# Two graph layers in one kernel: the second layer's weights, the sums of product 2 and the transpositions and projections of x in other places

## The chip, the cores and the metric

The kernel runs on one core of a Trainium2 chip. The metric is the time of one execution on the device in microseconds (us); several executions are taken and their median is given. A core has five engines that run their own instruction streams and wait for one another through semaphores: TensorE (PE; its weight loads are listed apart, as PEld), VectorE (DVE), ScalarE (ACT), GpSimd (POOL) and SyncE (SP), which here only issues DMA. SBUF is the memory on the core, PSUM the small one that PE writes its products to.

## What is computed

x has 16 batches of 1024 nodes and 64 channels, adj is 1024 x 1024; all is 32-bit floating point. Cut to what matters, the reference is:

```python
# layer 0
Q = einsum('bnc,oc->bno', x, Wq) + bq
K = einsum('bnc,oc->bno', x, Wk) + bk
V = einsum('bnc,oc->bno', x, Wv)
score = softmax(einsum('bnc,bmc->bnm', Q, K), axis=1)
score = einsum('bnm,mc->bnc', score, adj)
x = layernorm(x + einsum('bnm,bmc->bnc', score, V))
# layer 1, with support = adj twice
x1 = einsum('ij,bjk->bik', adj, x)
x2 = 2.0 * einsum('ij,bjk->bik', adj, x1) - x
out = concatenate([x, x1, x2, x1, x2], -1) @ weight + bias
x = layernorm(x + out)
```

The kernel multiplies adj with x first (the score matrix is then applied to that product), so there are three large products with adj: one ahead of the attention and two in layer 1. Since layer 1 uses the same support twice, its weights can be added up in front: that is `layer_weights`.

## The kernel before

**Products with adj.** Each large product is a Strassen product: seven products of half the size, numbered 1 to 7, with sums of blocks formed on DVE. Products 2, 3 and 4 are themselves cut into seven parts (`PARTS`, in the order 1, 2, 6, 5, 7, 3, 4). Sums that are needed later stand in a list, `line`; `fill(n)` emits the next n of them, `need(name)` all up to the last with that name. The order in which instructions are emitted is the order in which each engine runs its own. `step` is one half of a product of half the size, `part` one of the seven parts; both emit PE's matmuls, then some sums, then the reading of the PSUM tile.

```python
line = []

def later(name, pieces):
    line.extend((name, piece) for piece in pieces)

def fill(n):
    for _ in range(min(n, len(line))):
        line.pop(0)[1]()

def need(*names):
    while any(name in names for name, _ in line):
        fill(1)
# ... cut ...
    def read(self, name, g, rows=(0, 1)):
        pt = self.tiles[g if name in (1, 6, 7, 4) else 2 + g]
        for i, c in self.targets(name):
            self.take(
                pt[:, rows[0] * H : (rows[-1] + 1) * H],
                i * HB + 2 * g + rows[0], len(rows), c * NP // 2, NP // 2,
            )

    def step(self, name, g, fills=0, rows=(0, 1)):
        self.matmuls(name, g, rows)
        fill(fills)
        self.read(name, g, rows)
# ... cut ...
    def part(self, name, q, two_tiles, fills=1):

        a, b = self.sub[q]
        tile_, bank = {1: (0, 0), 6: (0, 0), 7: (0, 0), 4: (0, 0), 2: (1, 0)}.get(q, (1, 1))
        pt = two_tiles[tile_][:, ts(bank, H)]
        start = q in (1, 2, 5)
        W = H // 2
        for i in range(2):
            for k in range(2):
                nc.tensor.matmul(
                    pt[:, ts(i, W)], a[:, k, ts(i, P)], b[:, :, k],
                    start=(start and i == k == 0), stop=(k == 1), skip_group_check=True,
                )
        fill(fills)
        (i, c), = self.targets(name)
        di, dc = {1: (0, 0), 2: (0, 0), 6: (0, 1), 3: (0, 1), 7: (1, 1), 5: (1, 1), 4: (1, 0)}[q]
        self.take(pt, i * HB + 2 * di, 2, c * NP // 2 + 2 * dc, 2)
```

A reading adds to the result on DVE if the result's block has been written before, and copies on ACT if not. Products 5 and 7 have two targets each, so both engines read the tile.

```python
    def take(self, pt, block, n, pair, m):

        got = pt.rearrange("p (i q f) -> p q i f", i=n, q=m)
        cells = {(block + i, pair + q) for i in range(n) for q in range(m)}

        def at(t):
            return t[:, pair : pair + m, block : block + n]

        assert cells <= self.seen or not cells & self.seen
        if cells <= self.seen:
            nc.vector.tensor_add(at(self.res), got, at(self.res))
        elif self.plus is None:
            nc.scalar.activation(at(self.res), got, AF.Copy)
        else:
            nc.vector.tensor_add(at(self.res), got, at(self.plus))
        self.seen |= cells
```

**Transpositions, projections and weights.** The scores of layer 0 need x transposed (xT) and a projection of it (GY), for each of eight pairs of batches. Both go through a PSUM tile that ACT evicts.

```python
def transposed(p, pt=None):

    pt = ps_tile("pt") if pt is None else pt
    for k in range(K8):
        nc.tensor.transpose(pt[:, ts(k, P)], xs[:, p, k, :], ident)
    nc.scalar.activation(xT[:, p], pt, AF.Copy)

def score_weight(pw):
    nc.tensor.transpose(pw[:, 0:P], wq, ident)
    nc.tensor.transpose(pw[:, P : 2 * P], wk, ident)
    nc.vector.tensor_copy(wn, pw[:, 0 : 2 * P].rearrange("p (a o) -> p a o", a=2))

def score_weight_2(pm):
    nc.tensor.matmul(pm[:, 0:P], wn[:, 1], wn[:, 0], start=True, stop=True)
    nc.tensor.matmul(pm[:, H : H + 1], wn[:, 0], bkp, start=True, stop=True)
    nc.vector.tensor_copy(m_w, pm[:, 0:P])
    nc.vector.tensor_copy(gb, pm[:, H : H + 1])

def rows_of(p):
    return xs[:, p].rearrange("p k (b c) -> p (k b) c", b=2)

def project(p, pg=None):
    pg = ps_tile("pg") if pg is None else pg
    for h in range(2):
        nc.tensor.matmul(pg[:, ts(h, H)], m_w, xT[:, p, ts(h, H)], start=True, stop=True)
    nc.scalar.activation(GY[:, p], pg, AF.Identity, bias=gb, scale=1.0)
# ... cut ...
def layer_weights():
    w24 = const.tile([P, C], FP, tag="w24", name="w24")
    nc.vector.tensor_add(w24, w1s[:, 2], w1s[:, 4])
    nc.vector.tensor_sub(raw[:, 0], w1s[:, 0], w24)
    nc.vector.tensor_add(raw[:, 0], raw[:, 0], ident[:, 0:C])
    nc.vector.tensor_add(raw[:, 0], raw[:, 0], ident[:, C:P])
    nc.vector.tensor_add(raw[:, 1], w1s[:, 1], w1s[:, 3])
    nc.vector.tensor_scalar(raw[:, 2], w24, 2.0, None, op0=ALU.mult)
    rsum = const.tile([P, 5], FP, tag="rsum", name="rsum")
    nc.vector.tensor_reduce(rsum, raw, AX.X, ALU.add)
    nc.vector.scalar_tensor_tensor(
        raw, rsum[:, :, None].to_broadcast([P, 5, C]), -1.0 / C, raw, op0=ALU.mult, op1=ALU.add
    )
    wv = pair_weight("wv")
    for j in range(2):
        s = slice(j * C, (j + 1) * C)
        nc.vector.tensor_copy(wv[s, s], raw[s, 3])
    return wv
```

**The attention.** It takes 64 steps, eight for each of eight pairs of batches. `scores(n)` fills two PSUM tiles and DVE evicts them with their row maxima; ACT takes the exponentials; `scaled` divides the rows of the product of adj by the sums; `weighted` multiplies on PE. PSUM tiles of the pool `ps` come from three buffers in turn.

```python
const = ctx.enter_context(tc.tile_pool(name="const", bufs=1))
big = ctx.enter_context(tc.tile_pool(name="big", bufs=1))
small = ctx.enter_context(tc.tile_pool(name="small", bufs=4))
ps = ctx.enter_context(tc.tile_pool(name="ps", bufs=3, space=bass.MemoryType.PSUM))
pacc = ctx.enter_context(tc.tile_pool(name="pacc", bufs=1, space=bass.MemoryType.PSUM))
# ... cut ...
def scores(n):

    p, m = steps[n]
    sc = [ps_tile(f"sc{j}") for j in range(2)]
    for h in range(2):
        for j in range(2):
            s = slice(j * C, (j + 1) * C)
            nc.tensor.matmul(
                sc[j][:, ts(h, H)], GY[s, p, ts(m, P)], xT[s, p, ts(h, H)],
                start=True, stop=True,
            )
    NM[n] = small.tile([P, 2], FP, tag="nm", name="nm")
    E[n] = att.tile([P, 2, N], FP, tag="e", name="e", bufs=3)
    for j in range(2):
        nc.vector.tensor_scalar(
            E[n][:, j], sc[j], -1.0, None, op0=ALU.mult, op1=ALU.min,
            accum_out=NM[n][:, j : j + 1],
        )
    SM[n] = small.tile([P, 2], FP, tag="es", name="es")

def exponentials(n, j):
    nc.scalar.activation(
        E[n][:, j], E[n][:, j], AF.Exp, bias=NM[n][:, j : j + 1], scale=-1.0,
        accum_out=SM[n][:, j : j + 1],
    )

def scaled(n):

    p, m = steps[n]
    ri = small.tile([P, 2], FP, tag="ri", name="ri")
    nc.vector.reciprocal(ri, SM.pop(n))
    US[n] = small.tile([P, 2, C], FP, tag="us", name="us")
    nc.vector.tensor_tensor(
        US[n], U[:, m, ts(p, P)].rearrange("p (b c) -> p b c", b=2),
        ri[:, :, None].to_broadcast([P, 2, C]), ALU.mult,
    )

def weighted(n):
    p, m = steps[n]
    if m == 0:
        ACC[p] = pacc.tile([P, N], FP, tag="acc", name="acc")
    es, us = E.pop(n), US.pop(n)
    for h in range(2):
        for j in range(2):
            nc.tensor.matmul(
                ACC[p][j * C : (j + 1) * C, ts(h, H)], us[:, j], es[:, j, ts(h, H)],
                start=(m == 0), stop=(m == K8 - 1),
            )
```

```python
def centre(p):
    nc.gpsimd.tensor_tensor(
        rows_of(p), rows_of(p), mu[:, p, :, None].to_broadcast([P, G, C]), ALU.subtract
    )
```

**The main sequence**, as far as the change touches it. Of PSUM there are four tiles of two banks, h0 to h3 (`h`); `two` is h2 and h3.

```python
for n in (1, 2, 4):
    later(f"S{n}", left_sum(S, n))
for q in PARTS:
    first.part(2, q, two, {1: 0, 3: 2, 4: 2}.get(q, 1))
need("T1", "S1")
first.step(5, 0, 8)
need("S4")
later("half", both(*first.halves(3, room[0])))
first.step(5, 1, 8)
need("half")
later("T2", first.right_sum(2))
later("T3", first.right_sum(3))
later("S3", left_sum(S, 3))
for q in PARTS:
    first.part(3, q, two)
score_weight(h[3])
transposed(0, h[2])
need("T2")
lefts, rights = first.halves(4, room[1])
later("half", lefts)
later("mu", [
    lambda p=p: nc.vector.tensor_reduce(mu[:, p], rows_of(p), AX.X, ALU.add)
    for p in range(NP)
])
first.step(6, 0, 5)
score_weight_2(h[3])
transposed(1, h[2])
first.step(6, 1, 6)
project(0, h[3])
transposed(2, h[2])
need("S3", "T3")
line[:0] = [("T4", f) for f in first.right_sum(4)]
first.step(7, 0, 6)
project(1, h[3])
transposed(3, h[2])
line[:0] = [("half", f) for f in rights]
first.step(7, 1, 6)
project(2, h[2])
project(3, h[3])
need("T4", "half")
for q in PARTS:
    first.part(4, q, two)
    if q == 6:
        scores(0)
        for j in range(2):
            exponentials(0, j)
need("mu")
nc.vector.tensor_scalar(mu, mu, 1.0 / C, None, op0=ALU.mult)
nc.sync.dma_start(aT[:, low, right], a_in[:, low, right])
scores(1)
for j in range(2):
    exponentials(1, j)
transposed(4)
scaled(0)
wv = layer_weights()
for p in range(5):
    centre(p)
# ... cut ...
last = len(steps) - 1
for n, (p, m) in enumerate(steps):
    if (p, m) == (NP - 2, 2):
        later("half", both(*hop_1.halves(2, room[0])))
    if n + 2 <= last:
        scores(n + 2)
        exponentials(n + 2, 0)
    if p and m > 4:
        weigh(p - 1, m - 5)
    elif p > 1 and m == 0:
        weigh(p - 2, 3)
    elif p == 0 and m:
        if m % 2:
            project(m // 2 + 4)
        else:
            transposed(m // 2 + 4)
            centre(m // 2 + 4)
    if n + 1 <= last:
        scaled(n + 1)
    if m <= 4:
        fill(1)
    weighted(n)
    if m == K8 - 1:
        take(p)
    if n + 2 <= last:
        exponentials(n + 2, 1)
```

Of the kernel before, what the change touches and what calls it, by code (L numbers as in the profile page):

```python
# [18 lines left out]
def gnn_kernel(  # L19
# [31 lines left out]
    def ps_tile(name):  # L51
        return ps.tile([P, 2 * H], FP, tag="ps", name=name)
# [7 lines left out]
    def pair_weight(name):  # L60
        w = const.tile([P, P], FP, tag=name, name=name)
        nc.vector.memset(w, 0.0)
        return w
# [44 lines left out]
# [26 lines that stand above are left out]
# [14 lines left out]
# [18 lines that stand above are left out]
# [52 lines left out]
    def by_pair(t):  # L218

        return t.rearrange("p k (q f) -> p q k f", f=P)  # L220
# [4 lines left out]
# [10 lines that stand above are left out]
# [159 lines left out]
# [36 lines that stand above are left out]
# [19 lines left out]
# [4 lines that stand above are left out]
# [20 lines left out]
    def weigh(p, c, pw=None):  # L473

        pw = (ps_tile("pw") if pw is None else pw).rearrange("p (b f) -> p b f", b=2)
# [4 lines that stand above are left out]
                    pw[:, j, ts(k, 3 * C)], xT[s, p, ts(2 * c + k, P)],  # L480
                    raw[s, 0:3].rearrange("p w c -> p (w c)"), start=True, stop=True,
                )
        to = pw[:, :, 0 : 6 * C].rearrange("p b (k w c) -> p w k b c", k=2, w=3)
        blocks = slice(2 * c, 2 * c + 2)

        def at(t):
            return t[:, p].rearrange("p (k b c) -> p k b c", k=K8, b=2)[:, blocks]

        nc.scalar.activation(at(GY), to[:, 2], AF.Copy)  # L489
        nc.vector.tensor_tensor(  # L490
            at(xT), to[:, 0], raw[:, 4:5, None].to_broadcast([P, 2, 2, C]), ALU.add
        )
        nc.scalar.activation(
            U[:, blocks, ts(p, P)].rearrange("p k (b c) -> p k b c", b=2), to[:, 1], AF.Copy
        )

    def both(lefts, rights):
        return [f for pieces in zip(lefts, rights) for f in pieces]

    S = left_tiles()  # L500
    h = [ps_tile("h0"), ps_tile("h1"), pacc.tile([P, N], FP, tag="acc", name="h2"), ps_tile("h3")]
    two = h[2:]
    first = Product(S, xs, by_pair(U), h, None, (2, 3, 4))
# [7 lines left out]
    for n in (1, 2, 4):  # L511
        later(f"S{n}", left_sum(S, n))
    for q in PARTS:
        first.part(2, q, two, {1: 0, 3: 2, 4: 2}.get(q, 1))
    need("T1", "S1")
    first.step(5, 0, 8)
    need("S4")
# [6 lines left out]
    for q in PARTS:  # L524
        first.part(3, q, two)
    score_weight(h[3])
    transposed(0, h[2])
    need("T2")
    lefts, rights = first.halves(4, room[1])
    later("half", lefts)  # L530
# [2 lines left out]
        for p in range(NP)  # L533
    ])
    first.step(6, 0, 5)
    score_weight_2(h[3])
    transposed(1, h[2])
    first.step(6, 1, 6)
    project(0, h[3])
    transposed(2, h[2])  # L540
    need("S3", "T3")
    line[:0] = [("T4", f) for f in first.right_sum(4)]
    first.step(7, 0, 6)
    project(1, h[3])
    transposed(3, h[2])
    line[:0] = [("half", f) for f in rights]
    first.step(7, 1, 6)
    project(2, h[2])
    project(3, h[3])
    need("T4", "half")  # L550
# [11 lines left out]
        exponentials(1, j)  # L562
    transposed(4)
    scaled(0)
    wv = layer_weights()
    for p in range(5):
        centre(p)

# [7 lines left out]
# [8 lines that stand above are left out]
        elif p > 1 and m == 0:  # L584
            weigh(p - 2, 3)
        elif p == 0 and m:
            if m % 2:
                project(m // 2 + 4)
            else:
                transposed(m // 2 + 4)  # L590
                centre(m // 2 + 4)
        if n + 1 <= last:
            scaled(n + 1)
        if m <= 4:
# [6 lines that stand above are left out]
        if p:  # L601
            if m == 0:
                norm_1(p - 1)
            elif m == 1:
                norm_2(p - 1)
            elif m == 4:
                transposed(p - 1)
# [7 lines left out]
    h = [pacc.tile([P, N], FP, tag="acc", name="h0")] + [ps_tile(f"h{n}") for n in (1, 2, 3)]  # L615
# [8 lines left out]
    two = (h[2], h[3])  # L624
# [18 lines left out]
    two = (h[1], h[3])  # L643
# [136 lines left out]
```

## Time and profile before

| what | before |
|---|---|
| time, median of 3 runs | 621.12 us (620.71 to 621.95) |
| span of the profiled execution | 619.2 us |
| PE busy | 599.2 us (97%) |
| PE's weight loads busy | 305.0 us (49%) |
| DVE busy | 412.8 us (67%) |
| ACT busy | 232.8 us (38%) |
| POOL busy | 85.8 us (14%) |
| mean granted clock of PE | 0.986 |
| chain that ended last | PE 86%, DVE 6%, DMA 4%, ACT 2% |

How to read it. The profile is one execution, recorded by the hardware profiler. It has the busy time of each engine; the span in 40 equal slices, with a digit for the busy tenths of each engine and the clock that PE was granted; the chain of waits, followed back from the last instruction to what released each; groups of instructions by line; what each engine waited for (engine, tile, line, who was waited for, then us in total, times, longest); and a timeline. "L150" is line 150 of the kernel, and a line can be that of a helper: L299 and L301 are the two readings in `take`, L312 the matmuls of `step`, L375 those of `part`, L112 and L113 a transposition and its eviction, L132 and L133 a projection and its eviction, L401 and L408 the scores and their eviction, L415 the exponentials, L424 and L426 `scaled`, L438 `weighted`, L450 `centre`, L532 the sums for mu, L150 to L164 `layer_weights`. Matmuls in 32-bit floats stand in the trace as two instructions each. The share of busy time is a mean over stages with different limits, so a change is judged in its own stage.

### The profile page before, as it was taken

How to read it: one execution, taken by the hardware profiler on the slowest of the kernel's cores; microseconds unless marked ns; L12 is line 12 of the kernel's file. 1: busy time of each engine (PE TensorE's matmuls, PEld its weight loads, DVE VectorE, ACT ScalarE, POOL GpSimd, SP SyncE). 2: the span in 40 equal slices, each digit the busy share in tenths (PEclk: the TensorE clock that was granted, in tenths of full speed). 3: DMA queues.
4: the chain of work that ended last, by engine and by line, in shares of the span. 5: the costliest groups of instructions: out<-in, count | busy, mean ns of one | idle time of the engine just before them, and what ended most of it. 6: DMA issues, size and time to landing. Idle time of an engine off the chain costs nothing.

```text
span 619.2 us, 6448 instructions
## 1 busy us (share of the span) xinstructions
PE 599.2 (97%) x2478; PEld 305.0 (49%) x2478; DVE 412.8 (67%) x737; ACT 232.8 (38%) x384; POOL 85.8 (14%) x45
## 2 busy tenths in 40 slices
PE   9999999889999999999999999999999999999993
PEld 5747446423334434343443434446647466746463
DVE  0876565755586766778676787855768577648484
ACT  0111032236766667666667766662100000000111
POOL 0000000602130020303002030300000000203366
PEclk9999999969999999999999999999999999999997
DMA  8800002000000000000000000000000000000012
GB/s 264 292 7 1 0 0 69 0 0 2 1 1 1 0 1 2 1 1 0 1 2 0 2 0 1 1 1 1 1 0 0 1 0 1 1 34 35 34 68 103
DMA packets 12575, 14.34 MB, mean 23 GB/s; under 512 B 2304, under 2 KB 7424, under 8 KB 12544
## 3 DMA queue, kind: packets, MB, share of 16 engines
q1 hardware_dynamic: 12544, 13.93, 6.7%
q8 instruction: 19, 0.31, 0.2%
q14 instruction: 12, 0.10, 0.1%
HBM read 9.73 MB, written 4.19 MB: 22 GB/s over the span
## 4 chain that ended last, share of the span: by engine, by line
PE 86%; DVE 6%; DMA 4%; ACT 2%; SPq 1%; issue 1%; DVEq 0%; ACTq 0%
PE h L312 24%; PE sc L401 20%; PE acc L438 19%; PE h L375 13%; DMA xs<-in_x_dram 3%; PE pw L479 3%; PE po L458 2%; PE pt L112 2%; PE pg L132 2%; PE h L132 1%; DVE U L299 1%; DMA aT<-in_adjT_dram 1%; DVE GY L299 1%; DVE e L408 1%; PE h L112 1%; PE h L479 1%
## 5 line engine op out<-in xcount | busy, mean ns | idle before, releaser
L408 DVE TENSOR_SCALAR_CACHE_REDUCE e<-sc 128x1024 f32<-128x1024 f32 x128 | 151.7, 1222 | 64.5 <-PE sc L401 64.5
L415 ACT ACTIVATE e<-e,nm 128x1024 f32<-128x1024 f32 x128 | 146.2, 1143 | 94.7 <-DVE e L408 94.5
L401 PE MATMUL sc<-xT,GY 64*128 64x512 f32 x512 | 131.6, 621 | 4.9 <-DVE e L408 4.9
L438 PE MATMUL acc<-e,us 128*64 128x512 f32 x512 | 124.1, 605 | 0.3 <-DVE us L426 0.3
L175 POOL TENSOR_TENSOR rstd<-var,expo 128x16 f32<-128x16 f32 (+1 forms) x15 | 42.1, 2807 | 381.0 <-DVE var L170 381.0
L312 PE MATMUL h<-T,S 128*128 128x512 f32 x192 | 83.6, 593 | 0.9 <-DVE U L299 0.9
L401 PEld LDWEIGHTS sc<-xT,GY 64*128 64x128 f32 x512 | 45.7, 187 | 78.2 <-issue 46.5
L299 DVE TENSOR_TENSOR U<-h,U 128x512 f32<-128x512 f32 (+1 forms) x58 | 48.2, 837 | 53.1 <-PE h L312 30.2
L438 PEld LDWEIGHTS acc<-e,us 128*64 128x64 f32 x512 | 31.1, 136 | 70.0 <-issue 58.0
L703 ACT ACTIVATE sq<-GY 128x1024 f32<-128x1024 f32 x6 | 6.3, 1057 | 147.9 <-DVE GY L299 147.9
L312 PEld LDWEIGHTS h<-T,S 128*128 128x128 f32 x192 | 36.2, 190 | 44.5 <-issue 42.8
L312 PE MATMUL h<-S,aT 128*128 128x512 f32 x96 | 41.9, 592 | 0.0
L450 POOL TENSOR_TENSOR xs<-xs,mu 128x1024 f32<-128x1024 f32 x8 | 15.1, 1906 | 145.9 <-DVE mu L558 112.7
L375 PE MATMUL h<-xs 128*128 128x256 f32 x144 | 32.6, 382 | 1.4 <-DVE GY L299 1.1
L299 DVE TENSOR_TENSOR GY<-h,GY 128x512 f32<-128x512 f32 (+1 forms) x24 | 19.1, 798 | 16.7 <-PE h L312 11.2
L375 PEld LDWEIGHTS h<-xs 128*128 128x128 f32 x144 | 27.0, 190 | 6.2 <-DVE GY L299 1.5
L312 PEld LDWEIGHTS h<-S,aT 128*128 128x128 f32 x96 | 18.1, 190 | 22.0 <-issue 22.0
L301 ACT ACTIVATE U<-h 128x1024 f32<-128x1024 f32 x8 | 8.0, 1022 | 54.2 <-PE h L312 24.5
L479 PEld LDWEIGHTS pw<-raw,xT 64*128 64x128 f32 x224 | 19.2, 187 | 15.8 <-issue 5.8
L490 DVE TENSOR_TENSOR xT<-pw,raw 128x256 f32<-128x256 f32 x28 | 11.9, 425 | 18.6 <-ACT GY L489 18.6
L415 ACT ACTIVATION_READ_ACCUMULATOR e<-e,nm 128x1 f32 x128 | 24.0, 188 | 0.0
L479 PE MATMUL pw<-raw,xT 64*128 64x192 f32 x224 | 24.0, 332 | 0.0
(165 smaller groups left out, 625.4 us busy)
## 6 DMA issues: line engine op xcount, KB each, us to landing
xs<-in_x_dram SPq DMA_DIRECT2D x16, 256.0 KB, 5.8
aT<-in_adjT_dram SPq DMA_DIRECT2D x16, 256.0 KB, 5.5
out_dram<-GY SPq DMA_DIRECT2D x12, 256.0 KB, 2.2
aT<-in_adjT_dram SPq DMA_DIRECT2D x1, 1024.0 KB, 5.1
out_dram<-GY SPq DMA_DIRECT2D x8, 128.0 KB, 2.0
w1s<-in_w_dram SPq DMA_DIRECT2D x2, 80.0 KB, 2.7
wq<-in_wqT_dram SPq DMA_DIRECT2D x2, 16.0 KB, 4.7
wk<-in_wkT_dram SPq DMA_DIRECT2D x2, 16.0 KB, 3.8
```

Of the source, the lines that this page charges most:

```text
L112: nc.tensor.transpose(pt[:, ts(k, P)], xs[:, p, k, :], ident)
L132: nc.tensor.matmul(pg[:, ts(h, H)], m_w, xT[:, p, ts(h, H)], start=True, stop=True)
L175: nc.gpsimd.tensor_tensor(rstd, var, expo[:, 0:g], ALU.pow)
L299: nc.vector.tensor_add(at(self.res), got, at(self.res))
L312: nc.tensor.matmul(pt[:, ts(i, H)], a[:, k, ts(2 * g + i, P)], b[:, :, k], start=(start and k == 0), stop=(k == HB - 1), skip_group_check= ...
L375: nc.tensor.matmul(pt[:, ts(i, W)], a[:, k, ts(i, P)], b[:, :, k], start=(start and i == k == 0), stop=(k == 1), skip_group_check=True,)
L401: nc.tensor.matmul(sc[j][:, ts(h, H)], GY[s, p, ts(m, P)], xT[s, p, ts(h, H)], start=True, stop=True,)
L408: nc.vector.tensor_scalar(E[n][:, j], sc[j], -1.0, None, op0=ALU.mult, op1=ALU.min, accum_out=NM[n][:, j : j + 1],)
L415: nc.scalar.activation(E[n][:, j], E[n][:, j], AF.Exp, bias=NM[n][:, j : j + 1], scale=-1.0, accum_out=SM[n][:, j : j + 1],)
L438: nc.tensor.matmul(ACC[p][j * C : (j + 1) * C, ts(h, H)], us[:, j], es[:, j, ts(h, H)], start=(m == 0), stop=(m == K8 - 1),)
L450: nc.gpsimd.tensor_tensor(rows_of(p), rows_of(p), mu[:, p, :, None].to_broadcast([P, G, C]), ALU.subtract)
L479: nc.tensor.matmul(pw[:, j, ts(k, 3 * C)], xT[s, p, ts(2 * c + k, P)], raw[s, 0:3].rearrange("p w c -> p (w c)"), start=True, stop=True,)
```

## The change

It moves work and removes none.

- `layer_weights`, a dozen small instructions on DVE, goes from the beginning of the attention to a place behind the second step of product 7 of the first large product.
- In product 2 the sums that are emitted ahead of the readings go forward: two each ahead of the readings of parts 5 and 7 in place of parts 3 and 4. Their number is the same.
- The transpositions of pairs 0 to 3 go behind other steps of products 6 and 7; the projections of pairs 0 and 1 change place with some of them.
- In the steps of the first pair of the attention the transpositions of pairs 5, 6 and 7 go into steps 1, 3 and 5, and the projections of pairs 4 to 7 into steps 2, 4, 6 and 7. Before, the projections were in steps 1, 3, 5 and 7, the transpositions in 2, 4 and 6.

The aim is that small work of DVE stands where PE doesn't need DVE, and that PE meets fewer PSUM tiles that are still being read.

```diff
--- before.py
+++ after.py
@@ -511,7 +511,7 @@
     for n in (1, 2, 4):
         later(f"S{n}", left_sum(S, n))
     for q in PARTS:
-        first.part(2, q, two, {1: 0, 3: 2, 4: 2}.get(q, 1))
+        first.part(2, q, two, {1: 0, 5: 2, 7: 2}.get(q, 1))
     need("T1", "S1")
     first.step(5, 0, 8)
     need("S4")
@@ -524,7 +524,6 @@
     for q in PARTS:
         first.part(3, q, two)
     score_weight(h[3])
-    transposed(0, h[2])
     need("T2")
     lefts, rights = first.halves(4, room[1])
     later("half", lefts)
@@ -533,18 +532,20 @@
         for p in range(NP)
     ])
     first.step(6, 0, 5)
+    transposed(0, h[2])
     score_weight_2(h[3])
+    first.step(6, 1, 6)
     transposed(1, h[2])
-    first.step(6, 1, 6)
     project(0, h[3])
-    transposed(2, h[2])
     need("S3", "T3")
     line[:0] = [("T4", f) for f in first.right_sum(4)]
     first.step(7, 0, 6)
+    transposed(2, h[2])
     project(1, h[3])
     transposed(3, h[2])
     line[:0] = [("half", f) for f in rights]
     first.step(7, 1, 6)
+    wv = layer_weights()
     project(2, h[2])
     project(3, h[3])
     need("T4", "half")
@@ -562,7 +563,6 @@
         exponentials(1, j)
     transposed(4)
     scaled(0)
-    wv = layer_weights()
     for p in range(5):
         centre(p)
 
@@ -584,11 +584,11 @@
         elif p > 1 and m == 0:
             weigh(p - 2, 3)
         elif p == 0 and m:
-            if m % 2:
-                project(m // 2 + 4)
+            if m in (1, 3, 5):
+                transposed(m // 2 + 5)
+                centre(m // 2 + 5)
             else:
-                transposed(m // 2 + 4)
-                centre(m // 2 + 4)
+                project((m + 1) // 2 + 3)
         if n + 1 <= last:
             scaled(n + 1)
         if m <= 4:
```

## The prediction

> **What bounds the kernel now.** I read four views in this order: the page's 40 slices, the chain of waits, the timeline around the place that they point to, and the timeline of products 6 and 7. The slices say whether one engine is the bound and whether it keeps its clock; in the second row the clock that TensorE (PE) was granted stands in tenths.
>
> ```profile
> PE   9999999889999999999999999999999999999993
> PEclk9999999969999999999999999999999999999997
> ```
>
> PE is busy everywhere (97% of the span), so only three things can move the time: work of PE, gaps of PE, and its clock. One slice in the body of the kernel, the ninth (124 to 139 us), has a granted clock of about 0.6. The chain of work that ended last (start, length, what) passes there:
>
> ```profile
> 114.94 2.36 DVE e L408 x4
> ...
> 117.81 1.93 DVE w L150
> ...
> 119.77 1.83 DVE raw L151
> ...
> 121.69 1.76 DVE raw L152
> ...
> 125.60 1.25 DVE e L408 x2
> 126.84 0.04 issue
> 126.89 3.78 PE sc L401 x6
> 130.66 3.71 PE pg L132 x4
> 134.37 1.94 PE acc L438 x8
> 136.32 1.92 PE sc L401 x8
> 138.23 1.02 PE pt L112 x8
> 139.26 1.87 PE acc L438 x8
> 141.12 1.92 PE sc L401 x8
> 143.04 1.91 PE pg L132 x4
> ```
>
> Two things are to be seen. From 117.81 to 125.60 the chain runs through VectorE (DVE): these are the small instructions of `layer_weights`. Their place in DVE's order is ahead of the evictions of the third step's scores (e, L408). Those evictions free the PSUM buffers of the next scores, so PE stands still. Then, from 126.89, the same two PE groups that later take 1.92 and 1.91 us take 3.78 and 3.71. In stretches of the trace (length, busy time of PE, PEld, DVE, ACT, POOL, then the granted clock) this is:
>
> ```profile
> 121.60:126.90 5.30, 0.67 (x4) 0.02 (x2) 5.02 (x12) 0.03 (x1) 1.76 (x1) 0.75 0.00 0
> 126.90:134.50 7.60, 7.60 (x12) 2.52 (x14) 4.37 (x10) 3.68 (x7) 0.00 (x0) 0.50 0.00 0
> 136.25:141.05 4.80, 4.80 (x26) 2.02 (x24) 2.75 (x6) 1.86 (x5) 1.71 (x1) 1.00 0.00 0
> 141.05:146.75 5.70, 5.70 (x22) 1.85 (x20) 3.08 (x7) 4.17 (x7) 0.19 (x1) 1.00 0.01 3
> ```
>
> PE is nearly idle for 5.3 us and then works 7.6 us at half clock. The last two rows give the undisturbed beat of the first pair: 4.80 us for a step with a transposition, 5.70 for one with a projection, PE full in both. The list of what PE waited for in the whole run has only a few further entries of size; two of them are at places that the change touches:
>
> ```profile
> PE sc L401 <- DVE e L408: 4.9, 2, 4.6
> ...
> PE h L312 <- DVE U L299: 0.9, 1, 0.9
> ...
> PE h L112 <- DVE U L299: 0.6, 1, 0.6
> ```
>
> **What the Trainium skill says.** "TensorE: Matmul & The Clock Gate", Part 1 (The HAM clock gate): PE's clock falls to one half after an idle window of about 3.4 us and comes back after about as long a busy one. The trace agrees in kind: the idle stretch of some 5 us is followed by 0.50; but the half clock lasts to 134.5, that is 7.6 us of full work, longer than the page's figure. "SBUF — State Buffer", SBUF: two separate sides: a DVE instruction with two inputs in SBUF and a GpSimd (POOL) instruction reading SBUF share a port as an exclusive lock. The trace agrees: POOL runs its five `centre` instructions from 113.98 to 123.36, and L150, L151 and L152 (128x64) take 1.92, 1.82 and 1.75 us in that stretch, while L153 and L154, the same form right after it, take 0.23 and 0.22. "PSUM — Partial Sum Buffer", PSUM bank collisions: engines are to be kept from reading one bank at once, ScalarE (ACT) and DVE included. The trace agrees: in product 7 ACT's copy of a tile starts at 86.97, at the end of DVE's read of it (85.71 plus 1.23).
>
> **The change part by part.** It removes and adds no instruction; it reorders.
>
> **(a) `layer_weights` goes behind product 7's second step.** Gain: in the kernel before, the step from the scores at 121.14 to the next at 136.25 took 15.11 us and held scores, a projection and the weighted sum, 5.70 in the undisturbed beat. The loss is 15.11 - 5.70 = 9.4 us; of it 7.6/2 = 3.8 are the half clock, the rest the idle time. With the small instructions gone, DVE goes from the scaling (117.4 to 117.9) straight to the third step's scores, which PE has ready about 0.1 us after 119.27 (as the eviction at 138.26 follows PE's next start at 138.16). Two evictions of 1.15 us start to start and 1.22 long: the second buffer is free at 119.37 + 1.15 + 1.22 = 121.74, plus 0.06 to PE. PE wants it at 121.13. So a wait of about 0.65 stays, since the step before has neither transposition nor projection to fill it. Net gain 9.4 - 0.65 = 8.75. No half clock follows, as no long gap is left.
> Cost in the new place: from L153 to the end of the part the instructions took 125.60 - 123.48 = 2.1 us without POOL, and L150 to L152 add about 0.2 each, together 2.7 us in place of 7.8. After DVE's read in product 7 (95.17, next start 96.31) DVE does one sum for mu (1.21) and is then idle 3.09 until 100.61. 2.7 fits into 3.09. PE there works on projections and the last sub-product. Cost 0.
>
> **(b) Transposition 0 goes behind product 6's first step.** It stood right behind the last part of product 3, whose PSUM tile h2 it overwrites, and PE waited 0.56 for DVE's read. In the new place the read is long done, and product 6's step, which goes to h0, can start. Gain 0.56.
>
> **(c) Transposition 2 goes between product 7's first step and projection 1; transposition 3 follows and wants the same tile h2.** This makes a wait. With the old times: product 7's step ends near 85.5; DVE reads it until 86.94; ACT copies the other target from 86.97, its next instruction can start at 87.89, and that is now the eviction of transposition 2, 1.02 long, so h2 is free at 88.91. PE does transposition 2 (0.87) and projection 1 (1.72) from 85.51, so wants h2 at 88.10. Cost 0.85. ACT's copy is ahead in ACT's order, which is why the eviction can't go first. Transposition 1 and projection 0 behind product 6's second step find their buffers free.
>
> **(d) One more sum each ahead of the reads of parts 5 and 7 of product 2, one less ahead of 3 and 4.** Before the last read (part 4) two sums ran from 30.73 to 32.02, and the read began at 31.93; PE's part 4 began at 29.85 and a part takes 1.72, so the read could have begun 0.2 after 31.57, at 31.77. With one sum ahead of it DVE is waiting by then. The adjacency blocks that the earlier sums need had landed by 25.3. Gain 0.16, from the 0.94 that PE waits there; the rest of it is the end of part 4 and the read itself.
>
> **(e) Transpositions and projections of pairs 4 to 7 change places in the first pair's steps.** PE has 3 x 1.02 and 4 x 1.91 us in these seven steps in both orders; PE is the bound in them (DVE 2.75 to 3.08 us busy of 4.80 to 5.70). Worth about 0: the short transposition only meets the first step's wait earlier.
>
> Sum: 8.75 + 0.56 + 0.16 - 0.85 = 8.6 us. 621.1 - 8.6 = 612.5.
>
> **Rivals.** First, **the port lock takes the place of the wait**: `us` of the second step reads two SBUF inputs and, now earlier, falls into POOL's stretch up to 123.36, a delay of up to 1.5 us. For it: L426 took 0.47 and 0.63 beside POOL, against 0.29. Against it: PE needs `us` only after scores and a transposition, at about 124.7. If I am wrong there, another 1 us is lost: 613.5. Second, **the weights burden product 4**: if the 1.8 us of L150 to L152 were theirs and not the lock's, the part would take 7.8 us in a hole of 3.1, and the first read of product 4 would be some 4.7 late, of which PE has about 0.8 in hand; 616 or a little more, and a gap long enough to endanger the clock. The 0.23 of L153 speaks against it. Third, **the clock**: if the remaining short waits (0.3 and about 1 in the scores before, 0.65 after) together still brought the half clock, 3.8 of the gain would go, 616. PE's 0.94 wait in product 5 brought none. Fourth, **the wait of (c) doesn't come**, because ACT's order lets the eviction through earlier: 611.6.
>
> **Range and chances.** The gain of (a) is read from the trace and hardly less than 7.5; the small terms can be off by half a microsecond each, and the three runs before spread over 1.2 us. I take 611.0 to 614.5. Faster by over 2% would need 608.7, more than the whole loss that I find: 0.03. Slower by over 2% would need a new fault of 20 us: 0.01. Same: 0.96.
>
> **What would show it.** (a) The granted clock is 1.00 through the whole first pair; `layer_weights` lies near 96 to 99 us and takes about 2.7; L150 to L152 take about 0.2 each; PE's wait for e L408 falls from 4.9 to about 1. (b) No wait of L112 for U L299. (c) A new wait of PE's L112 for ACT, xT L113, of about 0.85 near 88 us. (d) PE's L312 waits for U L299 0.8 in place of 0.9. It would be wrong if the slow clock came again, or if PE waited in product 4 for DVE.

## The result, and the profile after

| | before | after |
|---|---|---|
| time, median of 4 runs | 620.99 us (620.71 to 621.95) | 612.07 us (611.82 to 612.36) |
| ratio | | 0.9854, 95% interval 0.9837 to 0.9871 |
| span of the profiled execution | 619.2 us | 610.0 us |
| PE busy | 599.2 us | 594.5 us |
| DVE busy | 412.8 us | 408.3 us |
| mean granted clock of PE | 0.986 | 0.994 |

The change made the kernel 8.9 us faster, 1.5%. In the slices of the page the ninth no longer has a lower clock; only the slow stretch at the very end is left:

```profile
PE   9999999999999999999999999999999999999993
PEclk9999999999999999999999999999999999999997
```

The chain of waits (start, length, what) at the beginning of the attention now consists of PE, but for one wait for DVE's eviction of the second scores:

```profile
115.22 1.23 DVE e L408 x2
...
116.49 1.12 PE sc L401 x2
...
117.63 1.98 PE sc L401 x6
119.61 1.87 PE acc L438 x8
121.48 1.92 PE sc L401 x8
123.40 1.02 PE pt L112 x8
```

The fourth scores begin at 121.48 and take 1.92 us in one piece, followed at once by the transposition. In the timeline of the kernel before they had begun at 121.14 and stopped after two of their eight instructions. The steps 1 and 2 together hold the same work in both kernels. The timelines give 121.14 to 141.05 before, 19.91 us, and 121.41 to 131.92 after, 10.51: 9.4 us less.

The weights stand in the timeline of DVE behind product 7's reading (start, length, line, operation):

```profile
96.59 0.22 DVE L150 TENSOR_TENSOR w<-w1s 128x64 f32<-128x64 f32 x1
...
97.17 0.23 DVE L152 TENSOR_TENSOR raw<-raw,ident 128x64 f32<-128x64 f32 x1
...
99.52 1.22 DVE L531 TENSOR_REDUCE mu<-xs 128x16 f32<-128x1024 f32 x1
100.89 0.69 DVE L299 TENSOR_TENSOR U<-h,U 128x512 f32<-128x512 f32 x1
```

L150 to L152 (L151 is left out here) take 0.22 or 0.23 us each where they took 1.75 to 1.92. The whole part takes 2.9 us (96.59 to 99.52), and the sum for mu ends at 100.74, 0.15 us ahead of the first reading of product 4. What PE waited for (us in total, times, longest):

```profile
PE h L312 <- DVE U L299: 0.8, 1, 0.8
PE h L112 <- ACT xT L113: 0.7, 1, 0.7
...
PE sc L401 <- DVE e L408: 0.3, 1, 0.3
```

The wait for e L408 fell from 4.9 to 0.3, the one of L112 for U L299 is gone, and one of L112 for ACT's eviction is new.

### The profile page after: what moved, and what is told of

Same layout as the page of the kernel before. It is cut to its first block, busy times and chain, and to the rows that moved or that the text cites. A ratio compares the mean times of both kernels' runs of the same rounds, so it can differ in the third digit from the quotient of the medians.

```text
span 610.0 us, 6448 instructions
## 1 busy us (share of the span) xinstructions
PE 594.5 (97%) x2478; PEld 303.7 (50%) x2478; DVE 408.3 (67%) x737; ACT 232.8 (38%) x384; POOL 85.8 (14%) x45
## 4 chain that ended last, share of the span: by engine, by line
PE 89%; DVE 5%; ACT 2%; DMA 2%; SPq 1%; issue 1%; DVEq 0%; ACTq 0%
PE h L312 24%; PE sc L401 20%; PE acc L438 19%; PE h L375 15%; PE pw L479 3%; PE po L458 2%; DMA xs<-in_x_dram 2%; PE pt L112 2%; PE pg L132 1%; DVE U L299 1%; PE h L132 1%; DVE GY L299 1%; SPq L77 1%; PE h L479 1%; ACT U L301 0%
## 5 line engine op out<-in xcount | busy, mean ns | idle before, releaser
L408 DVE TENSOR_SCALAR_CACHE_REDUCE e<-sc 128x1024 f32<-128x1024 f32 x128 | 151.6, 1222 | 62.7 <-PE sc L401 62.7
L401 PE MATMUL sc<-xT,GY 64*128 64x512 f32 x512 | 128.7, 615 | 0.3 <-DVE e L408 0.3
L299 DVE TENSOR_TENSOR U<-h,U 128x512 f32<-128x512 f32 (+1 forms) x58 | 48.2, 837 | 50.1 <-PE h L312 30.3
L299 DVE TENSOR_TENSOR GY<-h,GY 128x512 f32<-128x512 f32 (+1 forms) x24 | 19.1, 797 | 16.7 <-PE h L312 11.2
```

What stands on the lines that cost most here:

```text
L401: nc.tensor.matmul(sc[j][:, ts(h, H)], GY[s, p, ts(m, P)], xT[s, p, ts(h, H)], start=True, stop=True,)
L408: nc.vector.tensor_scalar(E[n][:, j], sc[j], -1.0, None, op0=ALU.mult, op1=ALU.min, accum_out=NM[n][:, j : j + 1],)
```

## The experiments

All times are medians; "before" is the kernel before in the same comparison.

| run | time | before | ratio (95%) |
|---|---|---|---|
| weights alone in the new place | 612.14 | 621.15 | 0.9847 (0.983 to 0.9864) |
| all but the weights | 621.23 | 621.15 | 1.0001 (0.9993 to 1.0009) |
| transposition 2 early | 611.36 | 621.15 | 0.9837 (0.9823 to 0.9851) |
| PE kept busy in the gap | 619.25 | 621.15 | 0.9964 (0.995 to 0.9978) |
| centring later | 612.48 | 621.23 | 0.9861 (0.9847 to 0.9874) |
| first pair in the old order | 612.00 | 621.23 | 0.9852 (0.9839 to 0.9866) |
| weights twice | 613.93 | 621.23 | 0.9886 (0.9872 to 0.9899) |
| transposition 5 in the wait | 609.83 | 621.23 | 0.9819 (0.9805 to 0.9832) |

**1. The weights alone.** The kernel before, with part (a) of the change only:

```diff
     first.step(7, 1, 6)
+    wv = layer_weights()
     project(2, h[2])
...
     scaled(0)
-    wv = layer_weights()
```

> The kernel before with one part of the change alone: the second layer's weights prepared behind product 7's second step. Theory: this part carries the whole gain, 5.3 us of standing still and 3.8 us of half clock, in all 9.4; so about 611.6 us, granted clock 1.00 in the first pair, and the small instructions of the weights at about 0.22 us each near 97 us. Rival (the parts need one another: without the transposition in step 1 and the earlier sums, a new wait for the scores' eviction takes its place): 613 to 616.

Measured: 612.14 us, 9.0 less than before. PE's waits in the first pair are down to 0.3 us and the half clock there is gone. In the chain of waits the fourth scores, which begin at 121.56, take 1.92 us again and the projection follows at once:

```profile
119.69 1.87 PE acc L438 x8
121.56 1.92 PE sc L401 x8
123.48 1.91 PE pg L132 x4
```

One moved line carries the gain, and it needs none of the other parts.

**2. All but the weights.** The changed kernel with the opposite edit, so the parts (b) to (e) alone.

> The changed kernel with the weights put back to the beginning of the attention; all else as changed. Theory: the other parts together are worth -0.56 (transposition 0) -0.15 (sums of product 2) +0.70 (wait ahead of transposition 3), about 0.0; so 621.0 us, with the half clock back for about 10 us. Rival (the short transposition in step 1 in place of a projection shortens the slow stretch): about 620, since 1.9 - 1.0 us less work falls into the half clock.

Measured: 621.23 us, with a ratio of 1.0001. The other parts cancel out, to within about half a microsecond. The stretches of this run (length, busy time of PE, PEld, DVE, ACT, POOL, then the granted clock) add something that was not expected:

```profile
121.40:126.80 5.40, 1.12 (x4) 0.29 (x2) 5.12 (x11) 0.00 (x0) 2.23 (x2) 1.00 0.00 0
126.80:133.60 6.80, 6.45 (x16) 3.03 (x18) 4.73 (x12) 4.36 (x7) 0.69 (x1) 0.50 0.00 0
```

PE stands still just as in the kernel before, but the clock falls only at 126.79, 0.4 us before PE goes on at 127.15. The clock records of the trace have it at half for 6.83 us, against 10.24 in the kernel before, whose first 2.6 us lay in the gap, where PE had no work that could become slower. So the length of the slow stretch in the record is not its cost; only the part with work in it counts, 7.6 us before and 6.5 here.

**3. Transposition 2 early.** The changed kernel, with its new wait taken away:

```diff
     project(0, h[3])
+    transposed(2, h[2])
     need("S3", "T3")
     line[:0] = [("T4", f) for f in first.right_sum(4)]
     first.step(7, 0, 6)
-    transposed(2, h[2])
     project(1, h[3])
     transposed(3, h[2])
```

> The changed kernel with transposition 2 put back ahead of product 7's first step, so that transposition 3 no longer overwrites a tile whose eviction waits behind ACT's copy. Theory: PE's wait of 0.70 us of the changed kernel goes and nothing takes its place: 611.4 us, 0.6 to 0.7 less than the changed kernel. Rival (PE then waits at the same place for product 7's reading or for projection 1's tile): 612.1, the same.

Measured: 611.36 us, and PE's wait for xT L113 is not in the list any more. Beside the changed kernel on one chip (experiment 9) the difference is 0.82 us. How the wait arose is seen in the timeline of the changed kernel:

```profile
85.45 1.02 ACT L301 ACTIVATE U<-h 128x1024 f32<-128x1024 f32 x1 [7.01 <-DVE U L299]
...
86.38 1.02 ACT L113 ACTIVATE xT<-h 128x1024 f32<-128x1024 f32 x1
...
87.45 1.09 PE L112 MATMUL h<-ident,xs 128*128 128x128 f32 x8 [0.70 <-ACT xT L113]
```

The eviction of transposition 2 stands behind ACT's copy of product 7, and that copy behind DVE's reading of the same tile. Transposition 3 can start only at 87.45, 0.05 after the eviction's end. Of the parts (b) to (e), (c) was the one that cost time.

**4. PE kept busy in the gap.** The kernel before; PE gets work without use while DVE prepares the weights:

```diff
+        if n == 0:
+            pg4 = ps_tile("pg")
+            for _ in range(20):
+                nc.tensor.matmul(pg4[:, 0:P], still, still, start=True, stop=True)
```

(The tile is then handed to projection 4, which overwrites it.)

> The kernel before, with 20 matmuls of zeros (128x128, into the tile that projection 4 overwrites later) put between the first weighted sums and the fourth scores, where PE stands still for DVE. The weights stay in their old place, so the wait stays; only PE is not idle in it. Theory: the clock fell because PE stood still; now it stays at 1.00, and the 3.8 us of half clock are saved: about 617.2 us. Rival (the half clock has another cause than this gap): 621.0, with half clock at the same place.

Measured: 619.25 us, so 1.9 less than before, half of what was expected. The clock did stay at 1.00, so the theory of its fall holds; the size came out otherwise. The chain of waits of this run shows why:

```profile
127.33 1.12 PE sc L401 x2
...
128.47 1.98 PE sc L401 x6
130.45 1.91 PE pg L132 x4
```

The scores stop a second time after two of their eight instructions, until the second eviction is over (it begins at 127.19 and takes 1.22). That is a fault of the edit. `ps` has three buffers in turn, and the tile taken early for the idle work is the third. It pushes the fourth scores on to the two buffers of the third scores, and they wait for both evictions, where those of the kernel before wait for the first only. The second stop put off the rest from 127.33 to 128.47, 1.14 us. The timeline has the step at 12.58 us (121.58 to 134.16) against 15.11 before; 15.11 - 12.58 + 1.14 = 3.7, near the 3.8 worked out for the half clock. This correction is worked out from the trace, not run.

**5. Centring later.** The kernel before, with the weights in their old place; only POOL's work is moved out of their way:

```diff
-    for p in range(5):
-        centre(p)
...
         weighted(n)
+        if n == 2:
+            for q in range(5):
+                centre(q)
```

> The kernel before, with the weights in their old place; only GpSimd's first five centring instructions are emitted two steps later, so that they no longer run beside the weights. Theory: L150 to L152 are slow because GpSimd holds the port; without it the weights take 2.7 us in place of 7.8, the scores' evictions begin near 120.5, PE waits for the second of them until about 122.9 in place of standing still to 126.9, and no half clock comes: 621.1 - 9.4 + 1.8, about 613.5 us. Rival (the small instructions are slow by themselves, or the wait is long enough for the half clock anyway): 617 to 621.

Measured: 612.48 us, 8.75 less than before, without touching the weights. The timeline of DVE, and the weight load with which PE goes on in the fourth scores:

```profile
117.70 0.22 DVE L150 TENSOR_TENSOR w<-w1s 128x64 f32<-128x64 f32 x1
...
118.29 0.23 DVE L152 TENSOR_TENSOR raw<-raw,ident 128x64 f32<-128x64 f32 x1
...
120.66 1.23 DVE L408 TENSOR_SCALAR_CACHE_REDUCE e<-sc 128x1024 f32<-128x1024 f32 x1
...
121.81 1.22 DVE L408 TENSOR_SCALAR_CACHE_REDUCE e<-sc 128x1024 f32<-128x1024 f32 x1
...
121.95 0.72 PEld L401 LDWEIGHTS sc<-xT,GY 64*128 64x128 f32 x5 [0.43 <-DVE e L408]
```

The same instructions in the same place take 0.22 and 0.23 us when POOL is not at work. (Why POOL's work makes them slow, by a shared port or otherwise, the run doesn't show.) So the root of the loss was less the place of the weights than their running beside POOL's `centre`. The fourth scores take 2.64 us in the chain of waits of this run in place of 1.92. Thus, by the traces, the weights alone in the way of PE cost 0.7 us, and beside POOL 9.4. The medians have the two remedies closer, 9.0 us gained in experiment 1 and 8.75 here, but from one comparison to the next they scatter by half a microsecond. The 1.0 us by which the run beat its expectation has the same reason as the wait that the prediction had too much (below).

**6. The first pair in the old order.** The changed kernel with part (e) undone.

> The changed kernel with the old order of transpositions and projections in the first pair's steps; all else as changed. Theory: these steps are full of PE work in either order, so 612.1 us, the same as the changed kernel. Rival (the short transposition in step 1 matters, since it comes where the evictions are late): some 0.5 to 1 us more.

Measured: 612.00 us, the changed kernel's time. Part (e) does nothing that these runs can see.

**7. The weights twice.** The changed kernel, with the load in the new place doubled:

```diff
     first.step(7, 1, 6)
+    layer_weights()
     wv = layer_weights()
```

> The changed kernel with the weights prepared twice behind product 7, so twice the load of VectorE in the new place. Theory: once, it fits into VectorE's idle time there to within a few tenths of a microsecond; the second 2.7 us come out of the first reading of product 4, which ends near 103.9 in place of 101.6, while PE wants its tile at 102.3: about 1.6 us more, 613.7 us. Rival (there is more room than that, PE is not touched): 612.1.

Measured: 613.93 us, 1.9 more than the changed kernel. PE's longest wait for a reading of DVE in the parts of products rose from 0.7 to 1.8:

```profile
PE h L375 <- DVE U L299: 3.0, 4, 1.8
```

The hole behind product 7 is deep enough for one preparation and little more. Of the 2.9 us that the second one takes, PE felt 1.9; the rest went into the 0.15 us that DVE and about 0.7 us that PE had in hand there (in the changed kernel the first reading of product 4 ends at 101.58, and PE takes the tile at 102.34).

**8. A version faster than both.** On top of experiment 3, the transposition of pair 5 goes into the wait that is left ahead of the third scores:

```diff
     scores(1)
+    transposed(4)
+    transposed(5, pacc.tile([P, N], FP, tag="acc", name="pt5"))
     for j in range(2):
         exponentials(1, j)
-    transposed(4)
     scaled(0)
-    for p in range(5):
+    for p in range(6):
         centre(p)
...
-            if m in (1, 3, 5):
+            if m == 1:
+                pass
+            elif m in (3, 5):
```

> A version meant to be faster than both: as the changed kernel, with transposition 2 ahead of product 7's first step, and with transposition 5 taken out of step 1 and put into the wait that is left ahead of the third scores (in the tile of the weighted sums, which is free there), ACT's evictions of transpositions 4 and 5 ahead of the second exponentials. Theory: the wait for the second eviction is there anyway and hides 0.9 us of PE work: 610.5 us. Rival (the exponentials come two microseconds later, and the weighted sums wait for them): 611.4 or more.

Measured: 609.83 us. The chain of waits, beginning with the two transpositions, is all PE:

```profile
114.44 1.90 PE pt L112 x16
116.33 2.55 PE sc L401 x8
118.88 1.87 PE acc L438 x8
```

The two transpositions fill most of the wait; the third scores still take 2.55 us in place of 1.92, since their second tile comes free late. The exponentials come later, and the weighted sums don't wait for them.

**9. The three versions side by side on one chip.**

> The changed kernel itself, beside the two versions below on one chip. Theory: 612.1 us, as measured first.

> The version with transposition 2 ahead of product 7's first step, again, beside the changed kernel: 0.7 us less than it, the wait that PE had ahead of transposition 3. Rival (the 0.7 between two separate comparisons was scatter): the same.

> The version with transposition 5 in the wait ahead of the third scores, again, beside the other two. By its trace the stretch from the second scores to the fifth is 1.0 us shorter than with transposition 2 alone; so 1.7 us less than the changed kernel, 1.0 less than the version above. The medians of separate comparisons said 1.5 for the latter; if that is right, something else beyond that stretch became shorter.

Measured: 611.55, 610.73 and 609.98 us (before: 621.17), with ratios of 0.9848 (0.9834 to 0.9861), 0.9832 (0.9819 to 0.9845) and 0.9821 (0.9807 to 0.9835). The steps are 0.82 and 0.75 us, 1.6 together, close to the 1.7 that the traces give. That experiment 8 seemed to gain 1.5 over experiment 3 was scatter between comparisons, which is about half a microsecond here.

## Why the prediction was right

612.5 us was predicted, 612.07 measured. Its steps one by one:

- **(a), the weights.** The gross gain of 9.4 us is what the two timelines give, and experiment 1 shows that it comes from this part alone. The new place cost nothing, as said: from projection 2 to the first scores the chains have 3.43 and 5.39 us in both kernels. The part took 2.9 us there where 2.7 were worked out. The split into idle time and half clock holds in kind: with PE busy the clock stayed up. In size it holds only with the correction of experiment 4.
- **The wait of 0.65 us that was to stay did not come.** This is the one step that was wrong, and it was wrong twice. First, it let the fourth scores wait for both evictions of the third. But the step before takes no third tile, so the turn of the three buffers moves on by one. The fourth scores get a buffer that is long free and the one of the first eviction, which in the changed kernel ended at 120.04 (118.81 plus 1.23), well ahead of 121.41. Experiment 5 shows it: there PE goes on at 121.95, after the first eviction (120.66 plus 1.23), while the second lasts until 123.03. The kernel before could have told: its fourth scores did start two instructions before they stopped, and went on when the first eviction was done (125.60 plus 1.23, against 126.89). Second, it had the evictions begin only when the third scores are complete, at 119.37. But those scores had themselves stopped in the middle, so that their first tile was complete ahead of the other. In the changed kernel its eviction begins 0.73 us before PE goes on to the weighted sums at 119.54:

```profile
118.81 1.23 DVE L408 TENSOR_SCALAR_CACHE_REDUCE e<-sc 128x1024 f32<-128x1024 f32 x1 [0.65 <-PE sc L401]
...
119.54 1.94 PE L438 MATMUL acc<-e,us 128*64 128x512 f32 x8
...
119.96 1.22 DVE L408 TENSOR_SCALAR_CACHE_REDUCE e<-sc 128x1024 f32<-128x1024 f32 x1
...
121.41 1.99 PE L401 MATMUL sc<-xT,GY 64*128 64x512 f32 x8
```

Even the second eviction was over at 121.18, so with either slip put right no wait is left. The first slip made the expectation of experiment 5 too high. That the sum came out near all the same is because the slip was in a small term of it.
- **(b), transposition 0.** 0.56 was predicted. The wait is gone from the list. From product 3's parts to the first scores the chains give 55.26 us before (48.70 to 103.96) and 55.43 after (48.80 to 104.23), so 0.17 more with (b) and (c) together; with 0.86 for (c) that leaves 0.7 for (b).
- **(c), transposition 3.** 0.85 was predicted. By starts, PE wanted the tile at 84.00 + 0.87 + 1.72 = 86.59 and began at 87.45, 0.86 later; taking it away brought 0.7 to 0.8. The list shows 0.70, since it counts from the end of the matmul before.
- **(d), the sums.** 0.16 was predicted; PE's wait ahead of product 5 fell from 0.94 to 0.78 in the timelines. It was not run alone, but all traces have it: from the third part of product 2 to the start of product 5 the four with the old order take 9.83 or 9.84 us, the nine with the new one 9.68 or 9.69, so 0.14 less. What comes ahead of that stretch scatters by more: it began at 22.84 before and at 23.08 after.
- **(e)** was worth nothing, as said.

With the 0.65 left out and 0.7 for (b), the sum is 9.4 + 0.7 + 0.14 - 0.86 = 9.4; less the 0.24 by which that stretch began later, this is the 9.2 between the two spans. Between the medians it is 8.9.

Of the rivals, the port lock did lengthen `us` of the second step to 0.63 us, ending at 121.93; PE needed it at 124.35 and didn't wait. The weights as a burden on product 4 came only when they were doubled. The slow clock did not come back.

## What to carry to other kernels

When small instructions in a chain are several times longer than others of the same form, look at what else runs at that time before moving them: here 0.7 us of honest cost had become 9.4 through a neighbour on another engine, a full stop of PE and its half clock. When work is moved into a hole of another engine, count the hole, and look for which buffer's release, in the order of the evicting engine, comes last at the new place; and when a tile is added or left out in a rotation, work out anew who waits for whom.

## What was not expected of the hardware

The granted clock fell at different points of the same gap: 2.0 us after PE had run dry in the kernel before (122.26, the end of its last matmul, to 124.25), and 4.3 us after it in experiment 2 (122.52 to 126.79). The slow stretches of 10.24 and 6.83 us are three and two times 3.41, which agrees with the free-running window that the Trainium skill names in "TensorE: Matmul & The Clock Gate", Part 1. But the fall after 2.0 us is earlier than the idle window of about 3.4 us that the page asks for, and from the end of the gap PE worked 7.6 and 6.5 us before the clock came back, about two windows where the page speaks of one. Half of that work, 3.8 and 3.2 us, is an estimate of what the slow clock cost in each. The wait of 1.8 us in experiment 7 brought no fall.
